# One activation-table set that holds both Ln and Exp, loaded ahead of five ScalarE stages

## The chip, the cores and the metric

The kernel runs on 1 core of one Trainium2 chip. The metric is the device time of one execution in microseconds (us); lower is better. All data is float32.

## The reference

Four layers follow each other on an image tensor x of shape (4, 128, 64, 64): 4 images b, 128 channels, which lie on the 128 partitions, and 4096 pixels. Only the parts below touch the change.

```python
# layer 2 (convolutional attention + MLP)
def _biasfree_ln(x, w):                      # over the 128 channels
    mu = mean(x, axis=1); var = mean((x - mu) ** 2, axis=1)
    return x / sqrt(var + 1e-5) * w
attn = softmax(qk, axis=1)                   # 32 x 32 per image, heads of _elgca_attn
h = gelu(conv1x1(m)); h = h + gelu(depthwise3x3(h)); m = conv1x1(h)   # _elgca_mlp
out = _elgca_attn(_biasfree_ln(x, ln1_w)) + x
out = out + _elgca_mlp(_biasfree_ln(out, ln2_w))

# layer 3 (selective state space model)
m      = sigmoid(illum_w . [x, illumination]); f_low = x * m
hidden = f_high * rsqrt(mean(f_high ** 2) + 1e-5) * rms_w             # RMS norm
xs, z  = split(in_proj(hidden)); xs = silu(causal_conv4(xs)); gate = silu(z)
delta  = softplus(dt_proj(x_proj(xs)[:8]) + dt_proj_b)
h_t    = exp(delta * A) * h_(t-1) + delta * B * xs                    # scan, both directions
out    = layer_norm(out_proj(y * gate)) * ln_w + ln_b + gamma * f_low
```

Layer 0 is an attention over 4096 positions and layer 1 two shift and two adder convolutions with batch norms; together they are three quarters of the time and the change leaves them alone.

## The kernel before

The program is written with a tile framework: the code issues instructions in program order, a scheduler then orders each engine's own stream, and semaphores carry the dependences between engines. Each of TensorE (PE), VectorE (DVE), ScalarE (ACT), GpSimd (POOL) and the DMA queue of SyncE (SP) works through its stream in order.

[...] the build puts a load in front of each activation whose function is not in the set that stands loaded. It takes one set for `Ln` and another for `Exp`, so a pair of `Ln` and `Exp` costs two loads each time. Such a load has the line of the activation that it was put in front of.

`Common.rstd` (lines 66 to 69) makes 1/sqrt(var + eps) as exp(-0.5 ln(var + eps)): an `Ln` at L68 and an `Exp` at L69. It is called from the batch norms of layer 1 (two times, one column each), and per block of 512 pixels from three norms:

- **Layer norms of layer 2** (`layernorm`, L520 to L532, called at L539 as "a" and at L606 as "b" for each image, 8 blocks k each). Per block: mean over channels as a matmul `pm` (L524), `xc = x - pm` on DVE (L526), Square on ACT (L527), mean of squares as a matmul `pv` (L529), Ln, Exp, and the product with w on DVE (L532). `xc` and `rs` have two buffers, the PSUM tag `mm` four. On PE the two matmuls of successive blocks alternate: pv of a block stands ahead of pm of the next. Then follow: after "a", matmul and Gelu into `x2` (L545, L548), a depthwise convolution on DVE (L557) with its Gelu (L558), the pooled keys and queries, the softmax (its Exp at L587), and the product with v (L599, L603); after "b", the MLP in two halves of four channel groups (Gelu at L627, L644, L655, last sum at L665). The scheduler moves the first three blocks of norm "a" of image b+1 up, ahead of the last Gelu (L655) of image b.
- **RMS norm of layer 3** (`layer3_prepare`, L753 to L762): Square (L757), matmul `pv` (L759), Ln, Exp, product on DVE (L762), 8 blocks per image. Ahead of it stands the sigmoid loop (L736 to L751): the matmuls at L743, L744 (one row of the illumination map `mr`, read by a DMA at L741) and L750, a Sigmoid (L746), DVE at L747 and L751, and a write of `low_d` (L748). After it come the input projection (L771, copied at L772), the convolution of four taps on DVE (L774, L777), and Silu (L779, L788).
- **Norm of the scan's output** (`finish`, L998 to L1026, one call per block of 512 pixels, 32 in all): y, xs and the gate are read back (L1006), two matmuls `py` each for two channel halves (L1008, L1009), DVE (L1010), matmul `po` (L1014), Square (L1016), matmul `pvo` (L1018), Ln, Exp, DVE (L1023), POOL (L1024, L1025) and the write of `out` (L1026). `po`, `pvo`, `py` and the scan's `mg` share two PSUM buffers; `po` is held until L1023 has read it. 24 of the calls lie inside the scan, after every third tile; the last 8 follow the scan.

**Softplus** (L804 to L828, 8 units of 1024 pixels by 128 channels per image): dv = matmul + bias (L811, L814), Abs (L816), Exp (L817), on DVE uu = 1 + e (L820) and its rounding error (L821), Ln (L822), two more DVE sums (L823, L824), a write of `delta_d` (L825), a POOL product (L827) and a write of `du_d` (L828). The scheduler runs the second half of it beside the next image's sigmoid loop.

**The scan** (`layer3_scan`) goes through 128 tiles of eight pieces: exp(delta A) on ACT (L945), the scan on DVE (L947), the sum of both directions on PE (`mg`, L962), its copy on ACT (L971), two products on POOL (L933, L975), sums on PE (L984); deltas and products come in by DMA (L925).

Of the kernel before, what the change touches and what calls it, by code (L numbers as in the profile page):

```python
# [39 lines left out]
def rows(ap):  # L40

    return ap.rearrange("p (r w) -> p r w", w=W)
# [7 lines left out]
class Common:  # L50


    def __init__(self, nc, pool):
        self.pool = pool
        self.ident = pool.tile([P, P], F32, name="ident")
        make_identity(nc, self.ident)
        self.ones = pool.tile([P, P], F32, name="ones")
        nc.vector.memset(self.ones, 1.0)
        self.mean = pool.tile([P, P], F32, name="mean")
        nc.vector.memset(self.mean, 1.0 / P)  # L60
        self.eps = pool.tile([P, 1], F32, name="eps")
        nc.vector.memset(self.eps, 1e-5)
        self.one_col = pool.tile([P, 1], F32, name="one_col")
        nc.vector.memset(self.one_col, 1.0)

    def rstd(self, nc, out, var):

        nc.scalar.activation(out, var, AF.Ln, bias=self.eps)  # L68
        nc.scalar.activation(out, out, AF.Exp, scale=-0.5)  # L69


def inner(x, b, k):

    return x[b][:, RB * k : RB * (k + 1), :]
# [414 lines left out]
def layer2(tc, cm, xp, ln1, ln2, dw_w, dw_b, qkvl_w, qkvl_b, fc1_w, fc1_b, pos_w, pos_b, fc2_w, fc2_b):  # L489
    nc = tc.nc  # L490
    NCH = 4
    with ExitStack() as ctx:
# [25 lines left out]
            nc.vector.tensor_scalar(diag[:, t, :], cm.ident, pww[:, 0, t : t + 1], None, ALU.mult)  # L518

        def layernorm(b, w, out, tag):  # L520
            for k in range(NB):
                src = inner(xp, b, k)
                pm = ps.tile([P, BK], F32, tag="mm", name=f"pm{tag}{b}_{k}")
                nc.tensor.matmul(pm, cm.mean, src, start=True, stop=True)  # L524
                xc = sb.tile([P, BK], F32, tag="xc", name=f"xc{tag}{b}_{k}")
                nc.vector.tensor_tensor(rows(xc), src, rows(pm), ALU.subtract)  # L526
                nc.scalar.activation(xc, xc, AF.Square)  # L527
                pv = ps.tile([P, BK], F32, tag="mm", name=f"pv{tag}{b}_{k}")
                nc.tensor.matmul(pv, cm.mean, xc, start=True, stop=True)  # L529
                rs = sb.tile([P, BK], F32, tag="rs", name=f"rs{tag}{b}_{k}")  # L530
                cm.rstd(nc, rs, pv)
                nc.vector.scalar_tensor_tensor(out(k), src, w, rows(rs), ALU.mult, ALU.mult)  # L532

        for b in range(B):
            x_all = xp[b]
            hp = big.tile([P, HP, HP], F32, tag="hp", name=f"hp{b}")
            nc.gpsimd.memset(hp[:, 0:HP:HP - 1, :], 0.0)
            nc.gpsimd.memset(hp[:, 1 : HP - 1, 0:HP:HP - 1], 0.0)
            layernorm(b, ln1_sb, lambda k: hp[:, 1 + RB * k : 1 + RB * (k + 1), 1 : 1 + W], "a")  # L539


# [42 lines left out]
            mx = sb.tile([P, 2], F32, tag="mx", name=f"mx{b}")  # L584
            nc.vector.tensor_reduce(mx[d, 0:1], pqk[d, :], AX.X, ALU.max, negate=True)
            ex = sb.tile([P, 32], F32, tag="ex", name=f"ex{b}")
            nc.scalar.activation(ex[d, :], pqk[d, :], AF.Exp, bias=mx[d, 0:1])  # L587
            nc.vector.tensor_reduce(mx[d, 1:2], ex[d, :], AX.X, ALU.add)
            ri = sb.tile([P, 1], F32, tag="ri", name=f"ri{b}")
# [14 lines left out]

            m = big.tile([P, H, W], F32, tag="m", name=f"m{b}")
            layernorm(b, ln2_sb, lambda k: m[:, RB * k : RB * (k + 1), :], "b")  # L606

            for half in range(2):
# [89 lines left out]
def layer3_prepare(  # L698
# [4 lines left out]
    with ExitStack() as ctx:  # L703
# [29 lines left out]
        for b in range(B):  # L733

            fh = big.tile([P, N], F32, tag="fh", name=f"fh{b}")
            for k in range(NB):  # L736
# [13 lines left out]
                nc.tensor.matmul(pg, alr, mr[:, 1, :], start=True, stop=True)  # L750
                nc.vector.scalar_tensor_tensor(rows(fh[:, c]), rows(pg), 1.0, src, ALU.add, ALU.mult)  # L751

            for k in range(NB):  # L753
                u = f"{b}_{k}"
                c = bass.ts(k, BK)
                sq = sb.tile([P, BK], F32, tag="sq", name=f"sq{u}")
                nc.scalar.activation(sq, fh[:, c], AF.Square)  # L757
                pv = ps.tile([P, BK], F32, tag="mm", name=f"pv3_{u}")
                nc.tensor.matmul(pv, cm.mean, sq, start=True, stop=True)  # L759
                rs = sb.tile([P, BK], F32, tag="rs", name=f"rs3_{u}")  # L760
                cm.rstd(nc, rs, pv)
                nc.vector.scalar_tensor_tensor(fh[:, c], fh[:, c], rw, rs, ALU.mult, ALU.mult)  # L762
# [26 lines left out]
                    nc.sync.dma_start(sz_d[b, mc, :, c], sz)  # L789


            for k2 in range(NB // 2):
                xd = sb.tile([NX, 2 * BK], F32, tag="xd", name=f"xd{b}_{k2}")
                for s in range(2):
                    c = bass.ts(2 * k2 + s, BK)
                    px = ps.tile([P, BK], F32, tag="mm", name=f"pxd{b}_{k2}_{s}")
                    for mc in range(2):
                        nc.tensor.matmul(
                            px[0:NX, :], xw[:, mc, :], xs[mc][:, c], start=(mc == 0), stop=(mc == 1)
                        )  # L800
                    nc.vector.tensor_copy(xd[:, bass.ts(s, BK)], px[0:NX, :])
                c2 = bass.ts(k2, 2 * BK)
                nc.sync.dma_start(xdbl_d[b, :, c2], xd)
                for mc in range(2):  # L804
                    u = f"{b}_{k2}_{mc}"
                    bias = dtb[:, mc : mc + 1]
                    shape = [P, 2 * BK]
                    dv = sb.tile(shape, F32, tag="dv", name=f"dv{u}")
                    for s in range(2):
                        pd = ps.tile([P, BK], F32, tag="mm", name=f"pd3_{u}_{s}")  # L810
                        nc.tensor.matmul(  # L811
                            pd, dtw[:, bass.ts(mc, P)], xd[0:DT_RANK, bass.ts(s, BK)], start=True, stop=True
                        )
                        nc.vector.tensor_scalar(dv[:, bass.ts(s, BK)], pd, bias, None, ALU.add)  # L814
                    ee = sb.tile(shape, F32, tag="ee", name=f"ee{u}")
                    nc.scalar.activation(ee, dv, AF.Abs)  # L816
                    nc.scalar.activation(ee, ee, AF.Exp, scale=-1.0)  # L817

                    uu = sb.tile(shape, F32, tag="uu", name=f"uu{u}")
                    nc.vector.tensor_scalar(uu, ee, 1.0, None, ALU.add)  # L820
                    nc.vector.scalar_tensor_tensor(ee, uu, 1.0, ee, ALU.subtract, ALU.subtract)  # L821
                    nc.scalar.activation(uu, uu, AF.Ln)  # L822
                    nc.vector.tensor_tensor(uu, uu, ee, ALU.subtract)  # L823
                    nc.vector.scalar_tensor_tensor(dv, dv, 0.0, uu, ALU.max, ALU.add)  # L824
                    nc.sync.dma_start(delta_d[b, mc, :, c2], dv)  # L825
                    du = sb.tile(shape, F32, tag="du", name=f"du{u}")
                    nc.gpsimd.tensor_tensor(du, dv, xs[mc][:, c2], ALU.mult)  # L827
                    nc.sync.dma_start(du_d[b, mc, :, c2], du)  # L828
# [240 lines left out]
def kernel(ctx: ExitStack, tc: tile.TileContext, i: dict, out: bass.AP):  # L1069
# [23 lines left out]
    with tc.tile_pool(name="xp", bufs=1) as xpool:  # L1093

        xp = residual(tc, xpool, bn2, x1d, y2d)
        layer2(
            tc, cm, xp, i["ln1_w"], i["ln2_w"], i["dw_w"], i["dw_b"], i["qkvl_w"], i["qkvl_b"],
            i["fc1_w"], i["fc1_b"], i["pos_w"], i["pos_b"], i["fc2_w"], i["fc2_b"],
        )
        layer3_prepare(  # L1100
            tc, cm, xp, maps_d.rearrange("i (b r) w -> i b (r w)", b=B), i["illum_w"], i["illum_wl"],
            i["illum_b"], i["rms_w"], i["in_proj_w"], i["conv_w"], i["conv_b"], i["x_proj_w"],
            i["dt_proj_w"], i["dt_proj_b"], i["alpha"], i["gamma3"], low_d, xs_d, sz_d, delta_d, du_d, xdbl_d,
        )
# [99 lines left out]
```

## Time and profile before

| what | value |
|---|---|
| median of 3 runs | 23555.58 us (23554.83 to 23556.7) |
| profiled execution, its own time | 23557.55 us |
| span in its trace, first to last instruction | 23555.8 us |
| busy PE, DVE, ACT, POOL | 21606.2, 20116.0, 19647.4, 3766.7 us |
| mean granted TensorE clock | 0.959 |
| layers 0, 1 and the residual | from 0 to about 17984 us |
| layer 2 | about 17984 to 19411 us |
| layer 3, preparation | about 19411 to 20218 us |
| scan, then the last 8 `finish` calls | 20218 to about 23440, to 23556 us |
| table loads on ACT | 366, of 1283 ns each |

The last column of a line in the list of groups is the idle time of the engine just before the group's instructions, with what ended it. In the timeline each line gives the start, the duration, the engine and the line, and in brackets the idle time before it. A matmul of float32 with 128x512 elements appears as two records; its end is modelled.

### The profile page before, as it was taken

How to read it: one execution, taken by the hardware profiler on the slowest of the kernel's cores; microseconds unless marked ns; L12 is line 12 of the kernel's file. 1: busy time of each engine (PE TensorE's matmuls, PEld its weight loads, DVE VectorE, ACT ScalarE, POOL GpSimd, SP SyncE). 2: the span in 40 equal slices, each digit the busy share in tenths (PEclk: the TensorE clock that was granted, in tenths of full speed). 3: DMA queues.
4: the chain of work that ended last, by engine and by line, in shares of the span. 5: the costliest groups of instructions: out<-in, count | busy, mean ns of one | idle time of the engine just before them, and what ended most of it. 6: DMA issues, size and time to landing. Idle time of an engine off the chain costs nothing. (4 is left out here: it accounts for less than half of the span.)

```text
span 23555.8 us, 348033 instructions
## 1 busy us (share of the span) xinstructions
PE 21606.2 (92%) x146624; PEld 7799.2 (33%) x146624; DVE 20116.0 (85%) x15018; ACT 19647.4 (83%) x13700; POOL 3766.7 (16%) x1710
## 2 busy tenths in 40 slices
PE   9999999999999999999999999999997567677777
PEld 4443333333333333333333333333332222222222
DVE  7887999999999999889999999999997665777776
ACT  5666999999999999899999999999996336555555
POOL 5662000000000000000000000000000000577776
PEclk9999999999999999999999999999998776899999
DMA  0000000000000000000000000000000002788876
GB/s 14 9 5 12 1 3 7 1 3 5 3 3 1 3 1 3 8 5 3 5 3 1 5 5 1 3 1 3 3 1 32 0 3 96 182 195 194 194 192 163
DMA packets 174504, 809.07 MB, mean 34 GB/s; under 512 B 22716, under 2 KB 23364, under 8 KB 102788
## 3 DMA queue, kind: packets, MB, share of 16 engines
q1 hardware_dynamic: 172356, 778.42, 13.0%
q8 instruction: 1146, 18.78, 0.3%
q10 hardware_dynamic: 576, 8.39, 0.1%
q14 instruction: 426, 3.49, 0.0%
HBM read 658.15 MB, written 128.58 MB: 33 GB/s over the span
## 5 line engine op out<-in xcount | busy, mean ns | idle before, releaser
L392 ACT ACTIVATE a1a<-a1pb,a1wn 128x2048 f32<-128x2048 f32 x4096 | 7793.2, 2001 | 198.3 <-PE a1pa L338 101.3
L392 ACT ACTIVATE a2a<-a2pb,a2wn 128x2048 f32<-128x2048 f32 x4096 | 7791.9, 1999 | 136.2 <-PE a2pa L338 94.0
L403 DVE TENSOR_SCALAR a2d<-a2pb,a2wa 128x2048 f32<-128x2048 f32 x4096 | 4993.4, 1281 | 212.9 <-PE a2pa L338 212.4
L403 DVE TENSOR_SCALAR a1d<-a1pb,a1wa 128x2048 f32<-128x2048 f32 x4096 | 4992.1, 1281 | 207.2 <-PE a1pa L338 206.9
L338 PE MATMUL a2pa<-a2a,a2pick 128*32 128x512 f32 x32768 | 4576.3, 593 | 31.5 <-ACT a2a L392 31.5
L338 PE MATMUL a1pa<-a1a,a1pick 128*32 128x512 f32 x32768 | 4569.2, 593 | 31.5 <-ACT a1a L392 31.5
L338 PE MATMUL a2pa<-a2d,a2pick 128*32 128x512 f32 x32768 | 4436.8, 594 | 46.3 <-DVE a2d L403 46.0
L338 PE MATMUL a1pa<-a1d,a1pick 128*32 128x512 f32 x32768 | 4434.3, 594 | 47.2 <-DVE a1d L403 46.9
L421 DVE SCALAR_TENSOR_TENSOR a1a<-a1pb,a1wa,a1a 128x2048 f32<-128x2048 f32 x1024 | 2406.1, 2350 | 323.6 <-ACT a1a L392 323.6
L421 DVE SCALAR_TENSOR_TENSOR a2a<-a2pb,a2wa,a2a 128x2048 f32<-128x2048 f32 x1024 | 2406.1, 2350 | 314.1 <-ACT a2a L392 314.1
L338 PEld LDWEIGHTS a2pa<-a2a,a2pick 128*32 128x32 f32 x32768 | 1489.1, 110 | 2370.1 <-issue 2061.7
L338 PEld LDWEIGHTS a1pa<-a1a,a1pick 128*32 128x32 f32 x32768 | 1486.9, 110 | 2370.7 <-issue 2045.3
L962 PE MATMUL mg<-h,ident 128*128 128x512 f32 x4096 | 1982.8, 634 | 298.1 <-ACT m L971 227.4
L338 PEld LDWEIGHTS a2pa<-a2d,a2pick 128*32 128x32 f32 x32768 | 1347.1, 109 | 2472.1 <-issue 1935.5
L338 PEld LDWEIGHTS a1pa<-a1d,a1pick 128*32 128x32 f32 x32768 | 1345.4, 109 | 2471.8 <-issue 1913.8
L947 DVE TENSOR_TENSOR_SCAN h<-da,h,dbu 128x1024 f32<-128x1024 f32 x768 | 1804.2, 2349 | 87.0 <-POOL dbu L933 4.7
L962 PEld LDWEIGHTS mg<-h,ident 128*128 128x128 f32 x4096 | 787.1, 201 | 1529.4 <-issue 856.9
L186 POOL TENSOR_TENSOR ssum<-ssum,et 128x512 f32<-128x512 f32 x960 | 1230.3, 1282 | 232.9 <-ACT et L181 166.1
L975 POOL TENSOR_TENSOR m<-m,C 128x2048 f32<-128x2048 f32 x256 | 1157.7, 4522 | 605.2 <-ACT m L971 435.9
L933 POOL TENSOR_TENSOR dbu<-du,B 128x2048 f32<-128x2048 f32 x256 | 1153.6, 4529 | 26.3 <-DMA du<-du_d 26.3
L151 ACT COPY et<-pe 128x512 f32<-128x512 f32 x1024 | 596.6, 583 | 591.6 <-PE pe L149 575.9
L149 PE MATMUL pe<-q,k 128*128 128x512 f32 x2048 | 1051.1, 596 | 8.6 <-DVE mx L159 8.1
(267 smaller groups left out, 13672.1 us busy)
## 6 DMA issues: line engine op xcount, KB each, us to landing
dl<-delta_d SPq DMA_DIRECT2D x256, 1024.0 KB
du<-du_d SPq DMA_DIRECT2D x256, 1024.0 KB
xs_d<-xs SPq DMA_DIRECT2D x8, 2048.0 KB
sz_d<-sz SPq DMA_DIRECT2D x64, 256.0 KB
delta_d<-dv SPq DMA_DIRECT2D x32, 512.0 KB
du_d<-du SPq DMA_DIRECT2D x32, 512.0 KB
y_d<-ye SPq DMA_DIRECT2D x64, 256.0 KB
yx<-xs_d SPq DMA_DIRECT2D x64, 256.0 KB
```

Of the source, the lines that this page charges most:

```text
L149: nc.tensor.matmul(pe, k[:, bass.ts(j, P)], unit[u, "q"], start=True, stop=True)
L151: nc.scalar.copy(et, pe)
L186: nc.gpsimd.tensor_tensor(unit[u, "sum"], unit[u, "sum"], at, ALU.add)
L338: nc.tensor.matmul(pa[s][32 * g : 32 * g + 32, :], pick[v][:, 31 - jj : 63 - jj], d[:, bass.ts(s, BK)], start=False, stop=False, skip_grou ...
L392: nc.scalar.activation(rows(at), view(t), AF.Abs, bias=wn[t][:, co : co + 1], scale=0.5 if g == q else 1.0,)
L403: nc.vector.tensor_scalar(rows(dt), view(t), wa[:, t, co : co + 1], None, ALU.max)
L421: nc.vector.scalar_tensor_tensor(at, view(MAX_TAP), wa[:, MAX_TAP, co : co + 1], at, ALU.max, ALU.add)
L933: nc.gpsimd.tensor_tensor(t, du, by_states(b, h)[0], ALU.mult)
L947: nc.vector.tensor_tensor_scan(t[:, cols][:, s], da[:, s], st[n, "dbu", h][:, cols][:, s], 0.0 if e % 4 == 0 else st["last"], ALU.mult, AL ...
L962: nc.tensor.matmul(pm, cm.ident, st[n, way, h][:, bass.ts(k, BK)], start=(way == 0), stop=(way == 1))
L975: nc.gpsimd.tensor_tensor(m, m, by_states(tiles[n][0], h)[1], ALU.mult)
```

## The change

A method `ln_and_exp` issues an explicit load of the set that has both functions. `keep_in_program_order` pins it behind the ACT instruction that the source issued last, so that the scheduler can't move it ahead of that one. It is called in front of each layer norm of layer 2, in front of the softmax's Exp, in front of the RMS norm loop and in front of the softplus loop. No call is put in the scan or in the batch norms. The build goes on putting in a load wherever the set that stands loaded lacks the next function.

```diff
+    def ln_and_exp(self, tc):
+
+        tc.keep_in_program_order(tc.nc.scalar.preload_act_table_set("natural_log_exp_and_others"))
...
         def layernorm(b, w, out, tag):
+            cm.ln_and_exp(tc)
             for k in range(NB):
...
             ex = sb.tile([P, 32], F32, tag="ex", name=f"ex{b}")
+            cm.ln_and_exp(tc)
             nc.scalar.activation(ex[d, :], pqk[d, :], AF.Exp, bias=mx[d, 0:1])
...
                 nc.vector.scalar_tensor_tensor(rows(fh[:, c]), rows(pg), 1.0, src, ALU.add, ALU.mult)
 
+            cm.ln_and_exp(tc)
             for k in range(NB):
                 u = f"{b}_{k}"
...
                     nc.sync.dma_start(sz_d[b, mc, :, c], sz)
 
 
+            cm.ln_and_exp(tc)
             for k2 in range(NB // 2):
                 xd = sb.tile([NX, 2 * BK], F32, tag="xd", name=f"xd{b}_{k2}")
```

In the streams of the two built programs the number of table loads falls from 366 to 106:

| part | loads before | loads after, the explicit ones among them |
|---|---|---|
| layer 0 and batch norms of layer 1 | 5 | 5, 0 |
| layer 2 | 143 | 41, 12 |
| layer 3, preparation | 152 | 60, 8 |
| scan and `finish` | 66 | 0, 0 |

The streams of PE and POOL are the same in both programs. Without the loads, ACT's stream is the same but in `layer3_prepare`, where the order of softplus, sigmoid and RMS norm instructions changes around the border between two images; DVE's changes there too (and in a few neighbouring pairs of layer 2), and on SP a few reads of `mr` (L741) and the write of `xdbl_d` (L803) move behind writes of `delta_d` and `du_d` (L825, L828).

## The prediction

> **What bounds the kernel now.** I read the page first (slices), then ACT's groups by form, a table of windows by stage, and the timeline of one block in each stage that has the loads.
>
> ```profile
> span 23555.8 us, 348033 instructions
> ...
> PE   9999999999999999999999999999997567677777
> ACT  5666999999999999899999999999996336555555
> PEclk9999999999999999999999999999998776899999
> ```
>
> The first 30 slices are layers 0 and 1, with PE, DVE and ACT nearly full; they have 5 loads, which stay. The last ten (5572 us, from 17984) hold the rest. No engine is full there: chains of waits bound them, and the PE clock sags. The question is thus which load stands in such a chain.
>
> ```profile
> L68 ACT ACT_TABLE_LOAD x129 | 165.5, 1283 | 16.9 <-PE pvo L1018 8.8 <-PE a2pa L338 5.9
> L69 ACT ACT_TABLE_LOAD x128 | 164.2, 1283 | 2.3
> L822 ACT ACT_TABLE_LOAD x29 | 37.2, 1283 | 0.5
> ```
>
> The idle time before the loads is about nothing: they follow ACT's own work directly.
>
> ```profile
> 18111.00:18150.00 39.00, 24.88 (x35) 8.53 (x36) 10.46 (x16) 35.70 (x41) 0.00 (x0) 0.72 0.00 0
> 19411.00:19457.00 46.00, 44.90 (x48) 12.84 (x46) 11.36 (x16) 10.61 (x15) 0.00 (x0) 0.50 0.13 47
> 20218.00:23440.00 3222.00, 2507.19 (x6471) 893.30 (x6472) 2431.97 (x1096) 1824.57 (x2231) 2362.71 (x559) 0.93 0.81 191
> ```
>
> Columns: stretch, length, busy PE, PEld, DVE, ACT, POOL, clock, DMA share, GB/s. A layer norm "b" (first row) keeps ACT busy 35.7 of 39 us. The sigmoid loop (second) is PE's, at half clock. The scan (third) is shared by all, with ACT at 57%.
>
> [...] the next activation starts 10 to 20 ns later, so I count 1.30 us. [...] In the trace every such pair pays two loads. [...] a pair of records lasts 1.12 us at clock 1.00 and 2.07 at 0.50.
>
> **The change part by part.** 260 loads of 1.30 us leave ACT, 338 us: the ceiling. The streams as built put the remaining loads where the functions really change, plus, for norm "a" of images 1 to 3, six loads in the first three blocks (moved ahead of the pinned load).
>
> *Layer norms, layer 2.* One block at full clock:
>
> ```profile
> 18130.61 0.61 ACT L527 ACTIVATE xcb<-xcb 128x512 f32<-128x512 f32 x1
> 18131.24 1.28 ACT L68 ACT_TABLE_LOAD   x1
> 18131.28 1.12 PE L529 MATMUL pvb<-xcb,mean 128*128 128x512 f32 x2 [1.54 <-ACT xcb L527]
> 18132.24 1.02 PE L524 MATMUL pmb<-x,mean 128*128 128x512 f32 x2
> 18132.54 0.69 ACT L68 ACTIVATE rsb<-pvb,eps 128x512 f32<-128x512 f32 x1
> 18133.24 1.28 ACT L69 ACT_TABLE_LOAD   x1
> 18133.30 0.69 DVE L526 TENSOR_TENSOR xcb<-x,pmb 128x512 f32<-128x512 f32 x1 [1.81 <-PE pmb L524]
> 18134.54 0.63 ACT L69 ACTIVATE rsb<-rsb 128x512 f32<-128x512 f32 x1
> 18135.07 0.61 ACT L527 ACTIVATE xcb<-xcb 128x512 f32<-128x512 f32 x1
> ```
>
> Square to Square is 4.46 us, all ACT: .61 + 1.28 + .69 + 1.28 + .63 less overlap. DVE's L526 ends at 18133.99 and its Square waits until 18135.07. Without loads ACT needs 1.9; what is late next is the ring Square → pv → pm → L526 → Square, since PE has pv ahead of the next pm: from pv to L526 2.02, L526 .69, steps .07, Square .61: 3.40 us. Gain 1.06 a block. At half clock the block before takes 5.33 (Squares at 18111.05 and 18116.38), the ring 5.20 (pv to L526 3.82): gain .1. So the clock decides. Before, each norm alternates: [...] One slow block, then seven: 5.2 + 7 x 3.4 = 29.0 for 39, so 10; all slow: 41.6, a loss of 2.6. I take 7.5 for each of four "b": 30. Norm "a" of image 0 (48 us, partly waiting for the residual): 9. For images 1 to 3 five blocks gain, less one slow block: 4 each, 12. Sum 51. What follows (Gelu's load, L548 or L627) stays, beside the product and the next matmul. The eight explicit loads at the softmax and ahead of norm "b" lie in ACT's wait of 21.8 us before L527 and in those for L585: nothing; without that cover 1.3 each.
>
> *RMS norm.*
>
> ```profile
> 19464.93 1.28 ACT L68 ACT_TABLE_LOAD   x1
> 19466.23 0.69 ACT L68 ACTIVATE rs<-pv,eps 128x512 f32<-128x512 f32 x1
> 19466.81 0.62 ACT L757 ACTIVATE sq<-fh 128x512 f32<-128x512 f32 x1
> 19467.45 1.28 ACT L69 ACT_TABLE_LOAD   x1
> 19468.74 0.63 ACT L69 ACTIVATE rs<-rs 128x512 f32<-128x512 f32 x1
> 19469.39 1.28 ACT L68 ACT_TABLE_LOAD   x1
> ```
>
> 4.46 us a block again, with no wait in it. Here the Squares run ahead and PE has one matmul a block (2.07 at worst, .75 on DVE), so ACT stays the bound at about 1.9. Of 16 loads an image, 20.8 us, some three are not won: the first waits for PE anyway, the last lie between copies, and some stay at the border. 12.5 x 1.30 = 16 an image, 64 in all. DVE's convolution, idle until the copies at L772 end, starts as much earlier.
>
> *Softplus.* Two units form a group in the last image: Abs at 20148.85 and 20169.62, 20.8 us. The Ln load is covered: after it ACT still waits 1.25 us for L821. The Exp load isn't. Two loads a group, 2.6 us; four groups 10.4 for the last image. In images 0 to 2 the second half runs beside the sigmoid loop, which PE bounds with eight blocks of 5.72 us at half clock (second row of windows: PE 44.9 of 46); its loads (L746, L817, L822) gain nothing. I take 7 each. Sum 31. The move on SP puts the map reads for block 3 and some later ones behind two writes, which wait for L824 and L827; behind them queue the L744 matmuls and the `low_d` writes. Three `mr` buffers and a PE that is late anyway cover it: 0, at most one such SP wait of 7 us an image.
>
> *Scan.* Its first load (L945) comes after the wait for `dl`: 1.3. In a `finish` inside the scan, the Ln load runs beside pvo (Square ends 22894.05, pvo 22896.06): covered. The Exp load (22896.81) is not, and holds `po`, hence `mg`, hence DVE's scan, which stood idle from 22891.2 to 22904.2. PE still has `mg` work until about 22898.6, where L1023, 1.3 us earlier, would now have released the rest, against 22899.57 before: 1.0 us. 24 x 1.0 = 24 if no other wait takes it; DMA moves at share .81 and the tiles are tied to it, so I take 20 (bounds -20 and +75: an unproven shift of phase against buffers and clock, .15 to .6 us a tile of 128, in either sense).
>
> *Last eight finishes.* Here the wait for pvo stands ahead of the load:
>
> ```profile
> 23485.02 1.12 PE L1018 MATMUL pvo<-sq,mean 128*128 128x512 f32 x2 [0.69 <-ACT sq L1016]
> 23486.22 1.28 ACT L68 ACT_TABLE_LOAD   x1 [1.26 <-PE pvo L1018]
> 23488.22 1.28 ACT L69 ACT_TABLE_LOAD   x1
> ```
>
> Both loads are exposed, 2.6 us of a cycle of 11 to 12.5. The next `py` waits for Ln, so it comes 1.3 earlier; its inputs, asked for at 23483.3 to 23486.1, keep the DMA full until 23490.3, which is next. I take 2.0 for seven and 2.6 for the last: 16.6.
>
> **Sum.** 51 + 64 + 31 + 1.3 + 20 + 16.6 = 184 us, 54% of the ceiling. The profiled execution took 23557.55 (span 23555.8 and 1.75 around it), so 23373.6; it lies 2.0 over the median, so I predict 23372.
>
> **The rivals.**
> - *The clock eats the layer norms.* All of them lock at half clock: 5.2 us a block for 3.4. [...] Against: in norm "b" of image 0 slow blocks before have the same 3.8 us run, and the next block is fast. The norms then give 0 for 51, and if the scan gives nothing either: 184 - 51 - 20 = 113, 23442. With one of both, about 23400. Chance .13.
> - *The scan tightens.* Shorter stalls keep DMA (idle at 22908 to 22910) fed; .6 us a tile is 75 for 20: 23315. Chance .10.
> - *The loads were cover.* Everything that they delay waits for something else, as in the sigmoid loop; under 47 us is left. Against: the block rows above show ACT without a wait. 23530. Chance .02.
> - *Slower.* The scan's phase tips the other way: `finish` frees `po` earlier, PE's waits shift, and PE falls to half clock more often (now .93). Price: a tile takes 25.0 us (3204/128); the other parts give 164, so it must lose 1.65 us, 6.6%, a tile to end slower by 47: 23605. For: the chain of waits there goes through PE and POOL. Against: nothing is added to the scan. Chance .02.
> - That the loads stay is excluded: the built stream has 106.
>
> **How the numbers follow.** Forecast .73, rivals .13, .10, .02, .02. The forecast's own range is 23325 to 23425 (norms 20 to 60, scan 0 to 50, last finishes 8 to 20, softplus 20 to 31). For 8 in 10 I reach to most of the second case and of the first: 23310 to 23435. A difference of .2% (47 us) is what a measurement can tell from none: faster .96, same .02, slower .02.
>
> **What would show it.** Layer norm "b": Squares 3.4 us apart and a window of about 30 us, clock near 1. RMS: Squares under 2 us apart, Exp right after Ln. Softplus of the last image: groups of about 18 us, with a wait for DVE ahead of Ln. Scan: no load, L1023 about 1 us earlier after Square. Last finishes: Exp right after Ln, cycles of 9 to 10 us, DMA without its pause. I'm wrong if norm blocks stay at 5.2, if the scan's length moves by over 75 us, or if the sigmoid loop speeds up.

## The result and the profile after

| | before | after |
|---|---|---|
| median, us | 23555.58 (23541.1 to 23562.96, 5 runs) | 23418.93 (23406.72 to 23427.68, 5 runs) |
| profiled execution, and its span | 23557.55, 23555.8 | 23406.72, 23404.9 |
| table loads | 366 | 106 |

The ratio is 0.9943, with a 95% interval of 0.9928 to 0.9957. That is 137 us by the medians and 151 by the two profiled spans, where the prediction had 184. The time lies inside its range, but not because its terms were right: two of them (softplus and scan, 52 us together with the scan's first load) brought nothing, and one (layer 2) brought 28 us more. The profiled execution after is the fastest of its five, 12 us under their median; the stretches below come from that one execution and from one before.

The page after, its first line and two rows of the slices:

```profile
span 23404.9 us, 347773 instructions
...
ACT  5666999999999999989999999999997224555554
PEclk9999999999999999999999999999998776899999
```

ACT's digits fall in the last ten slices only (an 8 ahead of them lies one slice further), and the clock's row is digit for digit what it was. The groups of loads, by form, show what is left: L68 is now the explicit load, L72 and L73 are the former L68 and L69.

```profile
L68 ACT ACT_TABLE_LOAD x20 | 25.7, 1283 | 0.4
...
L72 ACT ACT_TABLE_LOAD x14 | 18.0, 1283 | 6.1 <-PE a2pa L342 5.9
```

The same three stretches as before, one layer norm "b", the sigmoid loop and the scan, in the table of windows (columns as before):

```profile
18098.00:18128.00 30.00, 19.25 (x38) 7.05 (x38) 10.20 (x15) 16.65 (x25) 0.00 (x0) 0.93 0.00 0
19333.00:19378.00 45.00, 45.00 (x49) 13.37 (x48) 12.03 (x17) 10.65 (x17) 0.00 (x0) 0.50 0.13 48
20078.00:23300.00 3222.00, 2533.10 (x6443) 901.09 (x6444) 2432.02 (x1096) 1760.91 (x2177) 2357.28 (x558) 0.91 0.81 191
```

The norm takes 30 us for 39, ACT is busy 16.7 in it for 35.7, and its clock went up from 0.72 to 0.93. The sigmoid loop is unchanged. The scan has 64 us less of ACT in the same 3222 us, and its clock fell from 0.93 to 0.91. Stage by stage, from the first instruction of one stage to that of the next (a norm counts from its first Square) in both traces, in us:

| stretch, sum over the images | before | after | change | predicted |
|---|---|---|---|---|
| layer norms "b" | 160.7 | 120.7 | -40.0 | -30 |
| norm "a", image 0 | 49.3 | 37.7 | -11.7 | -9 |
| MLP to the end of norm "a", images 1 to 3 | 688.5 | 676.4 | -12.2 | -12 |
| end of norm "a" to the softmax's Exp | 229.0 | 213.7 | -15.3 | 0 |
| first sigmoid to the convolution's copies | 318.9 | 254.8 | -64.1 | -64 |
| first Abs to the next image's first sigmoid, images 0 to 2 | 153.8 | 159.9 | +6.1 | -21 |
| first Abs to the scan, last image | 93.1 | 88.1 | -5.1 | -11.7 |
| scan | 3204.4 | 3215.1 | +10.7 | -20 |
| last eight finishes | 131.6 | 110.7 | -20.9 | -16.6 |

The step behind norm "a" is led by the 16 records of the matmul L545 (L550 after). Before, in image 1, they ran at half clock, and DVE then waited for their last Gelu; after, at full:

```profile
18377.80 14.02 PE L545 MATMUL pq<-hp,qw 64*128 64x512 f32 x16
18392.58 2.28 DVE L563 TENSOR_TENSOR cs<-x 32x2048 f32<-32x2048 f32 x1 [4.36 <-ACT x L548]
```

```profile
18350.85 7.22 PE L550 MATMUL pq<-hp,qw 64*128 64x512 f32 x16
```

A block of norm "b" after, with Squares 3.42 us apart. ACT now waits for DVE ahead of the Square, and the ring Square, `pv`, `pm`, L531, Square sets the pace:

```profile
18109.98 0.63 ACT L532 ACTIVATE xcb<-xcb 128x512 f32<-128x512 f32 x1 [0.23 <-DVE xcb L531]
18110.66 1.12 PE L534 MATMUL pvb<-xcb,mean 128*128 128x512 f32 x2 [1.44 <-ACT xcb L532]
...
18112.68 0.69 DVE L531 TENSOR_TENSOR xcb<-x,pmb 128x512 f32<-128x512 f32 x1 [2.08 <-PE pmb L529]
...
18113.40 0.63 ACT L532 ACTIVATE xcb<-xcb 128x512 f32<-128x512 f32 x1 [0.23 <-DVE xcb L531]
```

The RMS norm of image 0, where the Ln of one block follows that of the last by 1.3 to 1.7 us and ACT does not wait:

```profile
19377.28 0.69 ACT L72 ACTIVATE rs<-pv,eps 128x512 f32<-128x512 f32 x1
19377.87 0.62 ACT L764 ACTIVATE sq<-fh 128x512 f32<-128x512 f32 x1
...
19378.96 0.69 ACT L72 ACTIVATE rs<-pv,eps 128x512 f32<-128x512 f32 x1
```

In the softplus the wait ahead of Ln is for DVE, and long. In the last image these waits add up to 30.4 us, for 15.6 before. L829 is L821 before; it takes 1.21 us alone and 2.76 here, beside POOL's product. First a unit of the last image before, then one of image 0 after:

```profile
20159.22 1.28 ACT L822 ACT_TABLE_LOAD   x1
20164.81 1.06 ACT L822 ACTIVATE uu<-uu 128x1024 f32<-128x1024 f32 x1 [4.31 <-DVE ee L821]
```

```profile
19463.11 2.50 POOL L835 TENSOR_TENSOR du<-dv,xs 128x1024 f32<-128x1024 f32 x1 [176.45 <-DVE dv L832]
...
19463.93 2.76 DVE L829 SCALAR_TENSOR_TENSOR ee<-uu,ee 128x1024 f32<-128x1024 f32 x1
...
19466.73 1.06 ACT L830 ACTIVATE uu<-uu 128x1024 f32<-128x1024 f32 x1 [6.32 <-DVE ee L829]
```

A finish inside the scan. The Exp follows the Ln, but the Square came late: PE's y sum waits 3.59 us for POOL, and then it and `po` run at half clock (1.92 and 2.08 us). A finish of before waits as well, but here its y sum (1.04 us) still had the full clock:

```profile
22064.11 1.04 PE L984 MATMUL y<-m,rows_of 128*32 128x512 f32 x2 [3.25 <-POOL m L975]
22065.08 2.02 PE L1014 MATMUL po<-yx,ow 128*128 128x512 f32 x2
```

```profile
21104.50 1.92 PE L992 MATMUL y<-m,rows_of 128*32 128x512 f32 x2 [3.59 <-POOL m L983]
...
21106.35 2.08 PE L1022 MATMUL po<-yx,ow 128*128 128x512 f32 x2
...
21108.46 0.60 ACT L1024 ACTIVATE sq<-po 128x512 f32<-128x512 f32 x1 [2.48 <-PE po L1022]
...
21112.34 0.75 DVE L1031 SCALAR_TENSOR_TENSOR rs<-po,lw,rs 128x512 f32<-128x512 f32 x1 [7.51 <-ACT rs L73]
```

One of the last eight finishes, where Ln starts as `pvo` ends and Exp as Ln ends:

```profile
23342.17 1.12 PE L1026 MATMUL pvo<-sq,mean 128*128 128x512 f32 x2 [0.69 <-ACT sq L1024]
23343.39 0.69 ACT L72 ACTIVATE rs<-pvo,eps 128x512 f32<-128x512 f32 x1 [1.28 <-PE pvo L1026]
23344.11 0.63 ACT L73 ACTIVATE rs<-rs 128x512 f32<-128x512 f32 x1
```

### The profile page after: what moved, and what is told of

Same layout as the page of the kernel before. It is cut to its first block, busy times and chain, and to the rows that moved or that the text cites. A ratio compares the mean times of both kernels' runs of the same rounds, so it can differ in the third digit from the quotient of the medians.

```text
span 23404.9 us, 347773 instructions
## 1 busy us (share of the span) xinstructions
PE 21561.9 (92%) x146624; PEld 7793.4 (33%) x146624; DVE 20131.0 (86%) x15018; ACT 19315.0 (83%) x13440; POOL 3763.5 (16%) x1710
```

## The experiments

My theory after the comparison has four parts. The clock gave layer 2 more than was counted. DVE, slowed by POOL, took the softplus over from ACT. In the scan a finish is held by PE ahead of the Square, where its y sum and `po` run at half clock (1.92 and 2.08 us above), and not by the loads, on which I take the scan's length not to hang; the run with the loads put back tests that. RMS norm and last finishes are as predicted. The rivals are written into each expectation.

### The parts one at a time

The new method is called from one place only: the layer norms and the softmax, or the RMS norm, or the softplus.

```diff
+            cm.ln_and_exp(tc)
```

> The table of Ln and Exp is loaded only in the layer norms and the softmax of layer 2; layer 3 is as before. My theory: layer 2 gives the whole of what it gave in the changed kernel, about 79 us (norms b 40, norm a of image 0 12, of images 1 to 3 12, and 15 from the end of norm a to the softmax, where PE arrives at full clock): 23477 us, with RMS norm, softplus, scan and tail as long as before to 3 us each. Rival, the prediction's sum: 51 us, 23505. A second rival: part of the 79 comes from elsewhere, and the scan's length moves by over 8 us although nothing of it is touched.

> The table is loaded only ahead of the RMS norm of layer 3. My theory: sigmoid loop and RMS norm are 64 us shorter in sum over the four images (16 each, the prediction's figure), nothing else moves: 23492 us. Rival: the earlier end of the RMS norm runs into the convolution and the copies behind it, which give some back when the softplus is not shortened too: 40 us, 23515.

> The table is loaded only ahead of the softplus; the scan and its finishes then have no loads either. My theory: the softplus of images 0 to 2 is no shorter (0 to +6 us in sum), since DVE, slowed beside POOL's product, sets the length of a unit; the last image gains 5; the scan is 0 to 11 us longer[...]; the tail is 21 us shorter. In all -10 to -25: 23530 to 23545. Rival, the prediction's sum: softplus 31, scan 21, tail 17, in all 69: 23487.

| alone | median, us | ratio, 95% interval | its own stretch | the rest |
|---|---|---|---|---|
| layer 2 | 23479.04 | 0.9964 (0.9952 to 0.9977) | -71.7 | scan -6.4 |
| RMS norm | 23485.53 | 0.9969 (0.9956 to 0.9981) | -69.0 | last finishes -4.5 |
| softplus | 23536.36 | 0.9990 (0.9984 to 0.9997) | -10.2 in the softplus, -9.8 beside it | scan +19.6, last finishes -20.6 |

Layer 2 gives its gain by itself; the 8 us missing from 79 are image 0's, where the clock fell to half 0.6 us into the matmuls behind norm "a" this time (13.42 us for 7.22). The prediction's 51 is refuted. The RMS norm alone gives even more than in the changed kernel. The softplus alone gives 21, not 69. That this is what was expected is in part luck: the scan was 20 us longer, for 0 to 11, and the softplus and the stretch beside it 20 us shorter, for at most 5.

The parts don't add up: 78.5 + 72.1 + 21.2 is 172 by the medians. Some 25 us of the difference lie from the first Abs of an image to the next image's convolution, where the second half of the softplus runs beside the sigmoid loop. Images 0, 1, 2: before 133.7, 133.8, 132.9; RMS alone 116.8, 116.7, 116.2; softplus alone 126.6, 126.6, 133.3; both 118.7, 121.8, 120.2. So the softplus's call gives 7 us an image in two of three while the RMS norm still has its loads, and takes 2 to 5 once it has none. In its 7 us are loads of the RMS norm: its new order on ACT pairs some of that norm's Ln and Exp, and the stretch from the first sigmoid has 21 loads for 26 in those two. The other 10 us of the difference no run took apart.

### What bounds the softplus

```diff
-                    du = sb.tile(shape, F32, tag="du", name=f"du{u}")
-                    nc.gpsimd.tensor_tensor(du, dv, xs[mc][:, c2], ALU.mult)
-                    nc.sync.dma_start(du_d[b, mc, :, c2], du)
+                    nc.sync.dma_start(du_d[b, mc, :, c2], dv)
```

> The changed kernel without POOL's product of delta and xs in the softplus (delta itself is written in its place, so the scan reads other values; the number and sizes of the writes are the same). My theory: with the loads gone DVE bounds the softplus, and POOL's product slows it (operations of 0.7 and 1.2 us take 2.0 and 2.8 to 3.2 beside it): a unit gets 1.5 to 2.5 us shorter, 8 to 15 us in the last image and 4 to 8 in each of the images 0 to 2: 23390-23400. Rival: ACT's chain of Abs, Exp and Ln bounds it, and nothing moves but the last write: 23416.

The kernel leaves out POOL's product and writes delta in its place. The median is 23383.55 us (0.9928, 0.9915 to 0.9940), somewhat below the expectation. Against the changed kernel, the last image's softplus is 7.1 us shorter (81.0 for 88.1), less than the 8 to 15 expected, and the stretches of images 0 to 2 from the first Abs to the next convolution by 5.3, 4.8 and 4.8, in the lower half of the 4 to 8; the scan (3220.8) was not shorter. The stretches of images 0 to 2 are no clean measure: the order on ACT changed there too, and each has two loads (2.6 us) fewer. The last image has the same loads in both, and L829 shows what changed:

```profile
L829 DVE SCALAR_TENSOR_TENSOR ee<-uu,ee x32: 1204/1214/1226, 19458.0 to 20037.5; 128x1024 f32<-128x1024 f32 x32
```

None of its 32 executions takes more than 1.23 us, where the changed kernel has up to 3.25. So ACT waits for DVE there, and POOL's product is part of the reason: up to the last unit's last DVE sum the image takes 69.6 us for 75.4, 0.7 a unit. What else a unit of some 9 us holds, a chain between DVE and ACT, no run took apart. In the unit of image 0 shown above, L829 beside a product of 2.50 us took 2.76, 1.55 longer than the 1.21 alone; why it does was not shown.

### The scan: the loads, the clock and the order on PE

First, two loads put back into every finish of the changed kernel:

```diff
+            tc.keep_in_program_order(nc.scalar.preload_act_table_set("natural_log"))
             nc.scalar.activation(rs, pv, AF.Ln, bias=cm.eps)
+            tc.keep_in_program_order(nc.scalar.preload_act_table_set("exp_and_others"))
             nc.scalar.activation(rs, rs, AF.Exp, scale=-0.5)
```

> The changed kernel with two loads put back into every finish, one ahead of Ln and one ahead of Exp, and nothing else. My theory: inside the scan the loads change where the finish waits, not how long three tiles take[...]: the scan stays within 5 us of the 3215 of the changed kernel; the eight finishes at the end get back the 17 to 21 us: 23437 us. Rival, the prediction's term: the scan loses 20 more, 23457. Second rival: the missing loads are what made the scan 11 us longer, and it goes back to 3204: 23427.

The median is 23401.14 us (0.9931, 0.9919 to 0.9944). Its runs, 23396.5 to 23406.4, all lie below those of the changed kernel. The last finishes got back 7.2 us and not 17 to 21 (their cycle is 9.3 to 10.5 us instead of 8.5 to 9.5: this load for Ln starts right after the Square and runs beside `pvo`, while that of the kernel before waited for `pvo`). The scan went back to 3204.8. My theory is wrong on that point and the second rival right on it, though the whole is below all three totals expected: the scan is faster with the loads. The edit had one side effect, a copy of y that stands elsewhere on ACT in six finishes. The other runs whose finishes differ in nothing but the loads don't have it and agree, one profiled execution each: with loads 3204.4, 3197.9, 3205.1 and 3215.0 us, with this run 3205 on the mean; without them 3215.1, 3224.0, 3220.8 and 3227.3, mean 3222.

Where the time goes is seen in DVE, which does the scan itself. In the middle of each of the 128 tiles, ahead of its fifth piece, it waits for PE's `mg`; in 24 of them this wait holds a finish. These waits in sum, in us:

| tiles | before | loads put back | changed kernel |
|---|---|---|---|
| 24 with a finish | 330.1 | 325.2 | 320.4 |
| 24 right behind these | 52.7 | 47.7 | 63.9 |
| the other 80 | 248.4 | 259.4 | 257.4 |

So the finishes did get shorter without loads, by 9.7 us in all, half of what was forecast; what made the scan longer lies behind them. In the five runs with loads the tiles behind a finish wait 47.7 to 52.7 us, in the four without 63.9 to 68.5. Two such tiles of the changed kernel:

```profile
21890.52 2.29 DVE L955 TENSOR_TENSOR_SCAN h<-da,dbu 128x1024 f32<-128x1024 f32 x1 [1.90 <-PE mg L970]
```

```profile
21966.71 1.94 PE L992 MATMUL y<-m,rows_of 128*32 128x512 f32 x8 [2.78 <-POOL m L983]
21968.58 3.78 PE L970 MATMUL mg<-h,ident 128*128 128x512 f32 x4
21970.69 2.29 DVE L955 TENSOR_TENSOR_SCAN h<-da,dbu 128x1024 f32<-128x1024 f32 x1 [3.71 <-PE mg L970]
```

In the first the clock was at 1.00. In the second, after PE's wait for POOL, it was at 0.50, and `mg` came 1.8 us later. Eleven of the 24 tiles wait over 3.3 us in the changed kernel, one before.

The same shows in the groups of three tiles, from one finish's L1023 to the next. Of 21 groups within an image, before has 1 of over 81.5 us, the loads put back 4, the changed kernel 10, the softplus alone 12. In the changed kernel nine take 78.2 to 78.4 us and ten 82.0 to 82.1, and these ten are just those whose first tile has the long wait, which is half of the difference. In the scan of this trace the clock is at half in 103 stretches, of 3.41 us (45) or 6.83 us (58); before, in 100, of 3.41 us (78) or 6.83 us (22).

In the finish itself, DVE's next scan starts 9.69 us behind the Square on the mean of 24, for 10.97: the 1.3 us of one load, where the prediction had 1.0. But from the end of DVE's last scan to the Square it takes 3.67 for 2.79, because y and `po` meet half clock in nearly every finish: 3.5 to 3.8 us in 22 of 24, where the kernel before has that in 8. Why the clock's drops fall there more often without the loads is not shown.

Next, PE is kept busy by issuing `po`'s first matmul three times more:

```diff
+            for _ in range(3):
+                nc.tensor.matmul(po, ow[:, 0, :], gated[0], start=True, stop=True)
             for c in range(2):
                 nc.tensor.matmul(po, ow[:, c, :], gated[c], start=(c == 0), stop=(c == 1))
```

> The changed kernel; in each finish the first matmul of po is issued three times more than needed (same operands, its last issue counts), so that PE is busy while it waits for POOL's product. My theory: the PE clock no longer drops there, y and po run at full clock, the time from the end of DVE's scan to the Square falls from 3.7 to about 2.3 us in all 24 finishes, and the groups of three tiles that took 82.0 us [...] take 78.3 [...]: the scan falls from 3215 to some 3175-3185, 23385 us. Rival: the clock is only a companion, the groups of 82.0 stay, and the scan is within 5 us of 3215. Second rival: the added matmuls hold up mg and the y sums by 1 to 2 us each, and the scan is 20 us longer.

The median is 23329.24 us (0.9903, 0.9890 to 0.9917). The scan falls by 102 us to 3112.9, far more than expected; the end of DVE's scan to the Square is 1.09 us in all 24, not 2.3. The mean clock of the scan was 0.95 for 0.91. The last finishes are 21 us longer, since the extra matmuls cost there what they cost. The edit had done two things: the scheduler also placed both matmuls of `po` ahead of the y sums, so that they no longer stand behind POOL. Two kernels tell these apart. Each puts ordering edges (no waits) on PE in the finishes inside the scan. In the first, which has the three matmuls too, `po`'s last matmul stays behind the first y sum, as in the changed kernel:

```diff
+                po2 = st.pop("po2", None)
+                if po2 is not None:
+                    tc.add_manual_dep(po2, yi.ins.name, ...)
```

In the second nothing is added but the edge the other way, the y sums behind `po`'s last matmul:

```diff
+                    tc.add_manual_dep(yi.ins, po2.name, ...)
```

> The changed kernel with po's first matmul three times more in the 24 finishes inside the scan, but PE's order held as in the changed kernel (one y sum ahead of po's last matmul). In the first warm finish the order had moved as well; this keeps the clock's part alone. My theory: the clock stays full, DVE's end to Square falls from 3.7 to 2.3 us, the groups of 82.0 go, and the scan falls by 24 times 1.4, to about 3180: 23385 us. Rival: the order made the whole gain; the scan is 3205 or more and the total 23405 or more.

> The changed kernel with both matmuls of po ahead of the y sums in the 24 finishes inside the scan, so that they don't stand behind POOL's product; no work is added. My theory: Square comes 1.5 to 2.5 us earlier, at full clock or at half, and the scan falls by 35 to 60 us, less than the 102 of the warm finish, since the clock still drops in PE's wait for POOL: 3155-3180, 23370 us. Rival: the groups [...] still take 78.3 or 82.0, and the scan is 3205 or more: 23410.

| scan without loads | median, us | ratio, 95% interval | scan | DVE's end to Square | Square to next scan |
|---|---|---|---|---|---|
| changed kernel | 23418.93 | 0.9943 (0.9928 to 0.9957) | 3215.1 | 3.67 | 9.69 |
| clock only | 23348.19 | 0.9911 (0.9898 to 0.9925) | 3153.8 | 1.70 | 9.10 |
| order only | 23322.64 | 0.9900 (0.9887 to 0.9914) | 3114.7 | -0.37 | 10.17 |
| both | 23329.24 | 0.9903 (0.9890 to 0.9917) | 3112.9 | 1.09 | 9.08 |

Both matter, and they overlap: the clock alone gives 61 us, the order alone 100, both 102. The clock-only kernel is the clean one of the two: ACT, DVE and POOL keep their order in the scan, the mean clock over the execution was 0.964 for 0.960, and its 61 us are what DVE's waits in the finishes lost (259.1 for 320.4). In the order-only kernel the Square also moved ahead of one exp(delta A) on ACT in all 24 finishes, so its gain is not PE's order alone; 85 of its 100 us lie in the finishes (235.3). Both gave more than expected, the order alone about twice as much. `po` ran at half clock (1.94 us), and its Square still starts before DVE's last scan ends:

```profile
21094.09 2.34 DVE L955 TENSOR_TENSOR_SCAN h<-da,h,dbu 128x1024 f32<-128x1024 f32 x1
21094.22 1.94 PE L1029 MATMUL po<-yx,ow 128*128 128x512 f32 x2 [1.71 <-DVE yx L1025]
21096.20 0.60 ACT L1033 ACTIVATE sq<-po 128x512 f32<-128x512 f32 x1 [1.46 <-PE po L1029]
```

Groups of 82 us are gone in all three (none of 21 over 81.5), also where the clock still drops (mean 0.93 in the scan of the order-only kernel).

Last, the loads of the kernel before with PE's part out of the way. Layer 2's norms are changed in the same kernel, for the next section.

```diff
+            for _ in range(3 if b < B - 1 else 0):
+                nc.tensor.matmul(po, ow[:, 0, :], gated[0], start=True, stop=True)
...
-                nc.tensor.matmul(pv, cm.mean, xc, start=True, stop=True)
+                for _ in range(2):
+                    nc.tensor.matmul(pv, cm.mean, xc, start=True, stop=True)
```

> The kernel before, all loads in, with two additions in separate stages: po's first matmul three times more in the 24 finishes inside the scan (as in the warm finish, not in the last eight), and the variance matmul of layer 2's norms twice (same result; the order of the norms' other work stays). Scan, my theory: with the clock out of the way, the loads of a finish cost what the prediction said of one load, 1.0 to 1.3 us in each of 24: about 3140 for the 3113 without loads. Rival: a finish's loads are covered there too, and the scan is within 5 us of 3113. Layer 2, my theory: PE leaves norm a at full clock, so that the step to the softmax falls from 57.7 to 53.4 us with all loads in, while norms b, bound by ACT, stay at 36 to 40. Rival: that step stays at 57.7. In all about 23475, or 23450 with the rival in the scan.

The scan takes 3149.0 us for the 3112.9 without loads, 36 us. Of these, 26 lie in the finishes, 1.07 in each from Square to the next scan (10.15 for 9.08). So the prediction's price of a load in a finish, 1.0 us, was right once nothing else holds the finish, and the rival is out; the other 10 us lie in other tiles and were not priced. The whole took 23573.93 us (1.0007, 0.9999 to 1.0016), 99 over the expectation, mostly because of layer 2's norms.

### The clock's part in layer 2

```diff
-                nc.tensor.matmul(pm, cm.mean, src, start=True, stop=True)
+                for _ in range(2):
+                    nc.tensor.matmul(pm, cm.mean, src, start=True, stop=True)
```

> The kernel before, all loads in, with the matmul of the mean in the layer norms of layer 2 issued twice (same result), so that PE is busy for 3 of 4.5 us of a block [...]. It tells the clock's part of layer 2's gain from the loads' part. My theory: norms b fall from 40 to about 36 us each (ACT bound at 4.46 a block), the step from the end of norm a to the softmax from 57.7 to 53.4 in images 1 to 3 as in the changed kernel: 30 to 45 us in all, 23515-23528. Rival: the loads themselves made all of the gain; the norms stay at 40 or grow, and the step to the softmax stays at 57.7: 23557 or more.

It doesn't answer the question: 23645.39 us (1.0037, 1.0024 to 1.0049). The extra matmul made the scheduler put the product with w ahead of the next subtraction on DVE, so Square waits for the last block's Exp, and a block takes about 6.0 us even at full clock; over 49 us of norm "b" of image 0 the clock was 0.73, for 0.72 over 39 us before. The second try, `pv` twice in the kernel above, kept the order, but the extra matmul lies in the ring from Square to Square, and norms "b" took 49 us on the mean. How the 10 us that a norm "b" gained divide between loads and clock is thus not measured. An estimate comes from blocks at full clock in both traces, 4.46 us before and 3.42 after: 1.04 a block for the loads alone, some 6 of the 10 us over the six such blocks of a norm after.

For the step behind norm "a" there is an answer, since in image 1 of that kernel the matmuls behind the norm began at full clock with all loads in, and in image 2 at half:

```profile
18401.14 3.71 PE L546 MATMUL pq<-hp,qw 64*128 64x512 f32 x8
18405.93 5.51 PE L546 MATMUL pq<-hp,qw 64*128 64x512 f32 x8 [1.08 <-ACT x L549]
```

```profile
18764.40 14.02 PE L546 MATMUL pq<-hp,qw 64*128 64x512 f32 x16
```

The step to the softmax took 54.1 us in the first and 57.9 in the second. The other way round, image 0 of the clock-only kernel has no loads there, but its matmuls took 13.25 us, and the step 58.4. In the changed kernel they took 7.22 and the step 53.4 to 53.5. So the 15 us are the clock's, with or without loads in the norm. It is not simply the clock at which the norm ends: in images 2 and 3 of the kernel before, and in image 0 of the clock-only kernel, the norm's last matmul ran at full clock and the drop came 0.1 to 0.8 us into the matmuls behind it. What sets off the drop was not shown.

### The sigmoid loop, and a kernel that beats both

```diff
-        iwr = cp.tile([1, P], F32, name="iwr")
+        iwr = cp.tile([P, P], F32, name="iwr")
+        nc.vector.memset(iwr, 0.0)
...
-                mr = sb.tile([1, 2, BK], F32, tag="mr", bufs=3, name=f"mr{u}")
-                nc.sync.dma_start(mr, maps_d[:, b, c].rearrange("(o i) n -> o i n", o=1))
+                mr = mrs[k % 3]
+                nc.sync.dma_start(mr[0:1], maps_d[:, b, c].rearrange("(o i) n -> o i n", o=1))
```

(`alr` likewise; `mrs` are three tiles of 128 rows, zeroed once.)

> The changed kernel with the one-row matmuls of the sigmoid loop (L744 and the one of pg) filled up to 128 rows with zeros: the result and the number of matmuls are the same. My theory: a matmul on one row does not count as work for the PE clock, which is why that loop stays at half clock although PE is 97% busy; with full rows it runs at full clock, a block takes about 3.5 us instead of 5.72, image 0's loop is 15 to 19 us shorter, those of the others, which share DVE with the softplus, 5 to 15: 23360-23390. Rival: the clock has another cause and the loop stays at 5.7: 23419. Second rival: DVE is the next bound at about 5 us a block: 23410.

The median is 23352.02 us (0.9912, 0.9899 to 0.9926). The window of image 0's loop now reads:

```profile
19345.00:19375.00 30.00, 26.84 (x60) 10.68 (x59) 15.32 (x22) 18.28 (x31) 0.00 (x0) 1.00 0.19 72
```

Clock 1.00 for 0.50, with the same matmuls. The stretches from the first sigmoid to the convolution are 23 us shorter in image 0 and 16 in the others, 72 in all, more than expected; the scan ran 12 us longer in this run. Full rows and the order-only scan together:

> The changed kernel with two things that gained alone: both matmuls of po ahead of the y sums in the scan's finishes (23323 alone), and the one-row matmuls of the sigmoid loop filled to 128 rows with zeros (23352 alone). They lie in different stages. My theory: they add up, 96 + 67 us off 23419: 23256, with the scan near 3115 and the four stretches from the first sigmoid to the convolution near 31, 50, 50 and 51 us. Rival: part of either was the scan's phase, which moved by 12 us in the run with full rows; then 23240 to 23245. Second rival: the softplus beside the sigmoid loop, DVE's, gives some of it back, and it ends above 23275.

The median is 23254.23 us (0.9870, 0.9854 to 0.9887), 165 below the changed kernel: they add up. The stretches are 31.1, 50.4, 50.4 and 50.8 us, as expected; the scan took 3135, 20 over the expectation.

## Why the prediction was right or wrong

- **RMS norm, 64: right**, 64.1. Where a profile shows an engine in back-to-back work, 12.5 loads of 1.30 us an image come off the time.
- **Layer norms, 51: too small by 28.** The ring of 3.40 us and "one slow block, then seven", 29.0 us a norm, were right (30.2); that the clock would hold over the seven was my estimate, and it was 0.93 over the norm. The step that failed is the one after it: "I take 7.5", a hedge between that and all slow; it measured 10. Norm "a" was right to 3 us. Missing altogether, and 15 of the 28, is the clock of the matmuls L545 behind norm "a": 12.0 to 14.0 us before, 7.2 after, with DVE's pooling waiting 4.36 us for their last Gelu before. I had put this step down as unchanged.
- **Softplus, 31 with the last image: wrong.** "Two loads a group, 2.6 us" came off ACT, but ACT was not what set the pace: with 15 loads fewer in the last image, its Ln waits for DVE 14.8 us longer. DVE carries one L801, two L814, L820, L821, L823 and L824 a unit, 6.5 us by their rows, POOL's product stretches one or two of them by up to 2 us, and ACT waits for it. Four units of images 0 to 2 take 38 to 41 us for 42. "Groups of about 18 us" are 23.5, 15.6 and 17.2 in the last image, for 22.1, 20.8 and 18.7 before. I had read the wait of 1.25 us for L821 as cover of one load, and not asked what DVE does in the rest.
- **The move on SP at 0: right.** No matmul of L744 waits for its map read in the trace after; before, two had waited 3.0 us together.
- **Scan, 20: wrong in sign**, +10.7 here and 17 by the means. "1.0 us a finish" was about right from Square on, 1.3. What failed is the condition, "if no other wait takes it". PE's y sum waits for POOL, the clock drops in that wait, and half clock meets y and `po` in 22 of 24 finishes for 8, which takes back 0.9 of the 1.3 us. Then the tile behind the finish waits longer for `mg`, at half clock: 11 us in sum in this pair of traces, 16 by the means, with more in the other tiles. This is the mechanism of the rival "slower", at 11 to 17 us for its 211. The rival "scan tightens" did not happen by itself, though order and clock show that 100 us were there.
- **Last eight finishes, 16.6: nearly right**, 20.9. Both loads were exposed in all eight; the DMA, which I let take 0.6 back in each, is seen ahead of six `py` with 0.3 to 0.9 us, 3.1 together.
- **The clock eats the norms: refuted.** The norm's clock is 0.93.

The misses are +28 in layer 2, -33 in the softplus and the scan's start, -31 in the scan and +4 at the end. That the sum is off by only 33 of 184, by the profiled spans, is in part their compensation.

## What to carry to other kernels

Removing a fixed cost from one engine is worth its length only where the trace shows that engine without waits up to the next stage; elsewhere sum the work of the engine that is next, including what a neighbour adds to it. Price a stage together with the matmuls that follow it (those behind norm "a" took 12.0 to 14.0 us or 7.2, by their clock), and look for waits in which PE stands ahead of a chain: issuing two matmuls ahead of such a wait was worth 96 us by the medians here, the 260 loads 137. In a loop of several engines, a shorter step can make the whole longer: compare every wait of the engine that carries the loop, not only the one in the step that was changed.

## What the runs showed of the hardware

- Matmuls with one row did not keep the clock up: the sigmoid loop, which has two of them to one of 128 rows, has PE busy 45.0 of 45 us at clock 0.50; with 128 rows, mostly zeros, the same loop runs at 1.00, with PE busy 26.8 of 30 us. A PE busy throughout thus had half the clock here, and one with pauses the full.
- The 64-row matmuls behind norm "a" kept PE busy for 14.02 us at a clock of 0.50 throughout. Whether the rows are the reason there was not tried.
- A load costs 1.28 us in all 366 cases, and the next activation starts 10 to 20 ns after it where nothing else holds it (270 of them), also behind loads that were put by hand ahead of Exp (10 and 20 ns in two finishes at the end).
- Beside POOL's product of 128 x 1024, DVE's L829 took up to 3.25 us for 1.21; without the product none of 32 took more than 1.23.
- The scan's groups in the changed kernel came at 78.2 to 78.4 or 82.0 to 82.1 us in 19 of 21 cases; with PE's order or idle time changed they spread from 72 to 79. What sets the two lengths is not shown.
